# Moving dense steps between the stages of a two-layer kernel, with a new order for its mixing part

## The chip, the cores and the metric

The kernel runs on one core of a Trainium2 chip. Its time is the device time of one execution in microseconds (us), the median of the runs. The core has five engines that work beside each other, each in the order of its own instruction list: TensorE (PE) for matrix products and transposes, VectorE (DVE), ScalarE (ACT), GpSimd (POOL), and SyncE (SP), which issues most transfers. They wait for each other through semaphores.

## What is computed

Four sequences of 512 tokens with 256 features pass through two layers, all in float32. Cut to what matters:

```python
xn = layernorm(x)
# layer 0: linear attention and a gene bank, both on xn
phi = lambda a: elu(a) + 1
x = x + (phi(q) * cumsum(phi(k) * v) / 4) @ Wo.T + bo
      + tanh(ex @ Wd.T) * rms(xn) * (ex @ Wu.T) * scale   # ex: the softmax of the 32 best of 512 logits, times genes
# layer 1: a gated running mean feeding a wide dense part; and experts
xn = layernorm(x)
w = exp(rms(k)); y = sigmoid(rms(q)) * cumsum(w * v) / (cumsum(w) + 1e-6)
u, g = split(y @ w_swiglu.T)                              # 2 x 1024 wide
x = x + xn + (u * silu(g)) @ w_out.T
      + shared_expert(xn)                                 # 352 wide
      + sum of the two best of 16 experts(xn), weighted   # 176 wide each
```

## The kernel before

Tokens come in 16 tiles of 128. The program has five stages.

**Mixing**, up to the routing. Everything of layer 0, and of layer 1 the running means and the routing scores, for five units: batch 0 in two halves, and batches 1 to 3 whole. Its order on PE, DVE, ACT and POOL is fixed when the program is built. Each piece of work is a small generator (`logit_stream`, `top_stream`, `kv_stream`, `gate_stream` and others) that names the engine and an assumed duration of its next step. The class `Order` keeps a clock for each engine and lets one step go at a time: among the steps that could begin within `PULL` (line 65) of the earliest, the one with the lowest rank (`RANKS`, line 69, a number for each kind of work and unit). `LEAN` (line 106) says per unit which of two engines does a step. `begin` decides whether the normalisation of layer 1 (line 374) runs on POOL or DVE; `rise` whether ScalarE and POOL (lines 626, 629) or DVE (line 634) multiply the gene part; `value` whether ScalarE or DVE scales the values (lines 861, 867); `inverse` whether the gate's division takes two reciprocals (line 966) and one multiply into `yT` (line 990) on DVE, or one reciprocal, with POOL's product (line 962) and two further products (lines 978, 979) ahead of the multiply at line 981; `dense=27` that in the first 27 dense chunks ScalarE and POOL make `hid` (lines 1240, 1243) in place of DVE (line 1246). POOL's wide add at line 822 adds the normalised rows to `xs`. The four engines follow this order exactly; the other stages are ordered by the framework.

**Dense chunks.** The dense part and the shared expert are cut into 88 chunks: 8 halves of 256 tokens, each with `NC` = 11 chunks (3 of the shared expert, 8 of the wide part). A chunk is four products into `gu` (line 1163), a Tanh (1209; 1233 in the mixing part), two DVE operations into `hid` (1211 and 1212; 1235 and 1246 in the mixing part), and two down products into the half's accumulator `acc` (1184). The downs of a chunk stand two chunks behind its products. When a half's eleven chunks are in, DVE adds `acc` to `xs` (line 1196, `sum_up`), and the next half can have the accumulator, of which there is one. Chunks fill TensorE where other work cannot: 42 (`UPTO`) in the mixing part, the rest in the stages that follow.

**Routing** (`route`, beside 5 chunks): a product with a triangle of ones, `stri` (made at line 1038, in memory that the mixing part gives free), counts tokens per expert; DVE works out each token's row (`slot`). **Scatters** (beside 18 chunks): POOL issues 32 indirect transfers of 128 rows each (line 1138) that sort the tokens by expert in DRAM. `together` deals the two out in proportion, and `paced` ties a transfer to the last down product that was recorded before it. Three chunks follow alone.

**Experts**: 19 pairs of row groups. A step of `experts` fetches sorted rows (line 1422), turns them on TensorE (1414), copies them on ScalarE (1428), and multiplies the pair before (up 1461, Silu 1469, DVE 1470, turn, down 1483), then stores the results (1494).

**Last stage**: the remaining 20 chunks. POOL gathers the two expert rows of each token tile (32 transfers, line 1610, paced), DVE adds each to `xs` (line 1621), and SyncE stores finished tiles (1625); the last two tiles are stored after the last `sum_up` (1630). Gathers and adds are spread over the steps by the two conditions at lines 1607 and 1618.

Of the kernel before, what the change touches and what calls it, by code (L numbers as in the profile page):

```python
# [17 lines left out]
P = 128  # L18
B, L, D = 4, 512, 256
NT = L // P  # L20
# [8 lines left out]
NTT = B * NT  # L29
# [15 lines left out]
def run_all(steps):  # L45
    for _ in steps:
        pass


def together(*streams):  # L50

    live = [[iter(steps), n, 0] for steps, n in streams]
    while live:
        s = min(live, key=lambda s: s[2] / s[1])
        s[2] += 1
        if next(s[0], live) is live:
            live.remove(s)


PE, DVE, ACT, POOL = "PE", "DVE", "ACT", "POOL"  # L60
# [1 line left out]
REACH = {PE: 0.2, DVE: 0.13, ACT: 0.15, POOL: 0.1}  # L62


PULL = {PE: 0.2, DVE: 0.02, ACT: 0.05, POOL: 0.1}

RANKS = dict(
    front=(-12, 14.5, -21, -10.5, -7.5),  # L70
    turn=(-35, -36, -36, -36.5, -31.5),
    logit=(10.5, 14, 25.5, 28, 26),
    top=(-11.5, 16, 15.5, 16.5, 26),
    gene=(-46.5, -21, -41.5, -40, -30.5),
    kv=(-2, 21.5, -7.5, -8.5, 17.5),
    q=(37.5, 43, 41.5, 50, 43),
    out=(-23.5, -22.5, -5.5, -6.5, -15),
    begin=(-23.5, -26.5, -27.5, -17.5, -15.5),
    rest=(9, -28.5, -9, 4.5, -27),
    weigh=(51.5, 51, 51.5, 50.5, 52.5),  # L80
    gate=(3.5, 4, -1.5, 4.5, 9.5),
    router=(32.5, 34, 26.5, 29, 33.5),
    dense=(49, 9.5, 2),
)


# [18 lines left out]

LEAN = dict(
    taken=(1, 0, 1, 1, 1),
    rise=(0, 0, 1, 0, 0),
    norm=(0, 1, 1, 1, 1),
    value=(1, 0, 1, 1, 0),  # L110
    inverse=(1, 1, 1, 0, 0),
    begin=(0, 1, 1, 0, 1),
    dense=27,
)


class Order:
# [67 lines left out]
    def run(self):  # L185
        while self.live:
# [6 lines left out]
            if not self.live:  # L193
# [6 lines left out]
                for j, (s, t) in enumerate(zip(ready, begin))  # L200
                if s.ask[0] == engine and t <= begin[first] + PULL[engine]
            ]
# [12 lines left out]
def tile_two_layers(  # L215
# [23 lines left out]
    nc = tc.nc  # L239
# [5 lines left out]
    xs = const.tile([P, B, NT, D], F32, name="xs")  # L245
# [7 lines left out]
    def paced(inst):  # L253

        tc.add_manual_dep(
            inst,
            beat[-1],
            mybir.DependencyInfo(mybir.DependencyClass.Sync, mybir.DependencyReason.DATA),
            reason="transfers spread over the dense parts",
        )  # L260
        return inst
# [873 lines left out]
    def scatter():  # L1135
        for k in range(2):
            for i in range(NTT):
                sc = G.indirect_dma_start(  # L1138
                    out=xrows,
                    out_offset=bass.IndirectOffsetOnAxis(ap=slot[:, k, i : i + 1], axis=0),  # L1140
                    in_=xn1[:, i // NT, i % NT],
                    in_offset=None,
                ).ins
                tc.declare_no_dep(sc, group="scatter", reason="no two tokens share a row")
                tc.add_to_no_dep_group("scatter", sc)
                paced(sc)
                yield
# [9 lines left out]
    NC = len(chunks)  # L1157
    made = {}

    def up_product(gu, ins, t0, gw, g0, uw, u0, m, which, dw, dc):  # L1160
        for k, (w, at) in enumerate(((gw, g0), (uw, u0))):
            for h in range(NH):
                T.matmul(  # L1163
                    gu[0:m, k],
                    w[:, h, at : at + m],
                    ins[which][:, h, t0 : t0 + HB],
                    start=(h == 0),
                    stop=(h == NH - 1),
                )

    def source(half):

        unit = (half // 2, half % 2 * 2)
        return (unit, 0) if unit in made else ((half // 2, 0), half % 2 * HB)
# [3 lines left out]
    def down(half, n, hid):  # L1178
        nonlocal acc
        m, dw, dc = chunks[n][4], chunks[n][6], chunks[n][7]  # L1180
        if n == 0:
            acc = ps_a.tile([P, 2, D], F32, name="acc")
        for t in range(2):
            mm = T.matmul(  # L1184
                acc[:, t],
                hid[0:m, t * P : (t + 1) * P],
                dw[0:m, dc],
                start=(n == 0 and t == 0),
                stop=(n == NC - 1),
                skip_group_check=True,  # L1190
            )
        beat.append(mm.ins.name)

    def sum_up(half):
        here = xs[:, half // 2, half % 2 * 2 : half % 2 * 2 + 2]
        V.scalar_tensor_tensor(here, acc, 0.5, here, ALU.mult, ALU.add)

    def dense(first, behind):

        for c in range(first, 2 * B * NC):
            half, n = divmod(c, NC)
            unit, t0 = source(half)
            m = chunks[n][4]
            gu = ps_d.tile([P, 2, HB], F32, name="gu")
            up_product(gu, made[unit], t0, *chunks[n])
            th = wd.tile([P, HB], F32, name="th", bufs=3)
            S.activation(th[0:m], gu[0:m, 0], AF.Tanh, scale=0.5)  # L1209
            hid = wd.tile([P, HB], F32, name="hid", bufs=4)  # L1210
            V.scalar_tensor_tensor(th[0:m], th[0:m], 1.0, gu[0:m, 0], ALU.add, ALU.mult)  # L1211
            V.tensor_tensor(hid[0:m], gu[0:m, 1], th[0:m], ALU.mult)
            behind.append((half, n, hid))
            if len(behind) > 2:
                half, n, hid = behind.pop(0)
                down(half, n, hid)
                if n == NC - 1:
                    sum_up(half)
            yield
        for half, n, hid in behind:  # L1220
            down(half, n, hid)
        sum_up(half)
# [93 lines left out]
    def weight_stream():  # L1316
# [10 lines left out]
        for transfer in incoming:  # L1327
            paced(transfer)
            c += 1
            if c < UPTO:  # L1330
                yield "wait", ("down", c)

    UPTO = 42
    kinds = mybir.EngineType
    with tc.manual_schedule(engines={kinds.PE, kinds.DVE, kinds.Activation, kinds.Pool}):

# [15 lines left out]
        order.add(more_constants(), RANKS["front"][0])  # L1352
        dense_streams(order, UPTO)
        for unit, (b, i0, nt) in enumerate(((0, 0, 2), (0, 2, 2), (1, 0, NT), (2, 0, NT), (3, 0, NT))):
# [5 lines left out]
        order.run()  # L1360
    mixing.close()
    dd = dense(UPTO, [])

    def d(n):
        return islice(dd, n), n
# [1 line left out]
    routing = ctx.enter_context(ExitStack())  # L1367
    together((route(), 6), d(5))
    routing.close()
    together((scatter(), 33), d(18))  # L1370

    run_all(islice(dd, 2 * NC - 19))

    held = ctx.enter_context(ExitStack())
    wx = held.enter_context(tc.tile_pool(name="wx", bufs=2))
# [10 lines left out]
    NP2 = (NFU + NMU) // XG  # L1386
# [109 lines left out]
    def experts():  # L1496

        _, regs = nc.values_load_multi_w_load_instructions(
            offs[0:1, NTF : NTF + 2 * NMU],
            engines=[mybir.EngineType.SP],  # L1500
            min_val=0,
            max_val=(NE - 1) * EW,
            skip_runtime_bounds_check_because=clamped,
        )
        for p in range(2):
            fetch(p)
        for s in range(NP2 + 2):
            if s + 2 < NP2:
                fetch(s + 2)
            if s % every == 2 and s // every < NMU // XG:  # L1510
                bring(s // every, regs)
            if 0 <= s - 1 < NP2:
                up_tile(s - 1, 0)
            if s < NP2:
                turn_in(s)
            if 0 <= s - 1 < NP2:
                up_tile(s - 1, 1)
            if s - 2 >= 0:
                down_pair(s - 2)
            if 0 <= s - 1 < NP2:  # L1520
                turn_hidden(s - 1)
            yield
# [70 lines left out]
                    V.scalar_tensor_tensor(here, y, cpair[:, k, n : n + 1], here, ALU.mult, ALU.add)  # L1593
                nc.sync.dma_start(out[n // NT, n % NT * P : (n % NT + 1) * P], here)

    together((experts(), NP2 + 2))
    weights.close()


# [5 lines left out]
    added = 0  # L1605
    for step, _ in enumerate(dd):
        while asked < 2 * NTT and 5 * asked <= 9 * step:
            n, k = divmod(asked, 2)
            paced(
                G.indirect_dma_start(  # L1610
                    out=ys[:, asked],
                    out_offset=None,
                    in_=yrows,
                    in_offset=bass.IndirectOffsetOnAxis(ap=slot[:, k, n : n + 1], axis=0),
                ).ins
            )
            asked += 1
        while added < 2 * NTT and 15 * added <= 32 * (step - 3):
            n, k = divmod(added, 2)
            here = xs[:, n // NT, n % NT]  # L1620
            V.scalar_tensor_tensor(here, ys[:, added], cpair[:, k, n : n + 1], here, ALU.mult, ALU.add)
            added += 1
            if added % 4 == 0 and added < 2 * NTT:
                b, i = divmod(n - 1, NT)
                nc.sync.dma_start(
                    out[b, i * P : (i + 2) * P].rearrange("(t p) d -> p t d", p=P), xs[:, b, i : i + 2]
                )
    assert asked == added == 2 * NTT
    for i in (NT - 2, NT - 1):
        nc.sync.dma_start(out[B - 1, i * P : (i + 1) * P], xs[:, B - 1, i])  # L1630

# [54 lines left out]
```

## Time and profile before

| | us |
|---|---|
| median of 3 runs (526.8 to 528.15) | 526.89 |
| the profiled execution | 527.08 |
| its span, first to last instruction | 525.4 |
| TensorE busy | 506.4 |
| VectorE busy | 346.5 |
| ScalarE busy | 238.0 |
| GpSimd busy | 197.7 |
| granted TensorE clock, mean | 0.994 |

The stages stand in the span about so: mixing to 296, routing to 308, scatters and dense steps to 362.5, experts to 465, last stage to the end. In a row of the timeline the first number is the start, the second the duration, both in us; then engine, line, operation, what is written and read, and in brackets how long the engine stood idle before it and what ended that. PE is TensorE's products, PEld its weight loads. The ends of products are modelled, and consecutive ones overlap in the rows.

### The profile page before, as it was taken

The page shows a single profiled execution, that of the slowest core. Times are in us where ns is not written, and L with a number is a line of the kernel's source. Part 1 is how long each engine was busy: PE and PEld are TensorE (multiplying, and loading weights), DVE is VectorE, ACT ScalarE, POOL GpSimd, SP SyncE. Part 2 cuts the span into 40 slices and gives each one's busy share as a digit, 9 for nine tenths or more (in the row PEclk, how much of TensorE's full clock was granted, in tenths as well). Part 3 has the DMA queues.
Part 4 walks back from the last instruction along what each step waited for, and adds up shares of the span by engine and source line. Part 5 has one row for each costly group of instructions (what it writes and reads, how often), then busy time and mean ns, then how long its engine had stood idle before and what let it go on. Part 6 is the DMA issues. An engine that isn't in the chain of part 4 may idle for free.

```text
span 525.4 us, 7219 instructions
## 1 busy us (share of the span) xinstructions
PE 506.4 (96%) x2352; PEld 371.8 (71%) x2352; DVE 346.5 (66%) x938; ACT 238.0 (45%) x539; POOL 197.7 (38%) x229
## 2 busy tenths in 40 slices
PE   7899999999999999999899999999999999999895
PEld 5555575565676787678578888887776767688784
DVE  5899989999899799859559783333222222226653
ACT  2864896668757845873381111113333333311110
POOL 1713076364745566477220126660000000026562
PEclk8999999999999999999999999999999999999998
DMA  7999000000000000006516203245237345114442
GB/s 213 351 378 327 1 1 1 1 1 2 0 1 1 1 1 1 1 1 181 151 48 183 100 30 139 92 185 182 88 100 289 102 154 196 61 61 130 130 122 83
DMA packets 38920, 53.71 MB, mean 102 GB/s; under 512 B 4096, under 2 KB 33888, under 8 KB 38624
## 3 DMA queue, kind: packets, MB, share of 16 engines
q1 hardware_dynamic: 35104, 44.82, 25.2%
q0 software_dynamic: 3072, 8.39, 4.9%
q8 instruction: 20, 0.33, 0.3%
q14 instruction: 20, 0.16, 0.1%
q10 hardware_dynamic: 704, 0.01, 0.1%
HBM read 27.12 MB, written 18.61 MB: 87 GB/s over the span
## 4 chain that ended last, share of the span: by engine, by line
PE 62%; DVE 17%; POOL 8%; issue 5%; ACT 3%; DMA 2%; SPq 0%; POOLq 0%; ACTq 0%; DVEq 0%
PE gu L1163 16%; PE pu L1461 9%; PE acc L1184 8%; PE py L1483 6%; PE pm L877 6%; POOL ys L1610 5%; PE pm L413 4%; PE pt L1414 3%; PE pm L456 3%; DVE rep L560 3%; DVE top L558 2%; PE pm L380 2%; DVE sums L966 1%; PE pm L483 1%; PE pm L489 1%
## 5 line engine op out<-in xcount | busy, mean ns | idle before, releaser
L1163 PE MATMUL gu<-yT,wugt 128*128 128x256 f32 x512 | 120.4, 379 | 0.0
L1163 PEld LDWEIGHTS gu<-yT,wugt 128*128 128x128 f32 x512 | 96.3, 190 | 13.4 <-issue 0.8
L1610 POOL DMA_INDIRECT ys<-yrows,slot x32 | 30.5, 952 | 129.1 <-PE gu L1163 111.9
L1184 PE MATMUL acc<-wot,hid 128*128 128x256 f32 x256 | 66.0, 383 | 2.3 <-DVE hid L1246 1.4
L1209 ACT ACTIVATE th<-gu 128x256 f32<-128x256 f32 (+1 forms) x46 | 17.6, 383 | 103.9 <-PE gu L1163 61.6
L1184 PEld LDWEIGHTS acc<-wot,hid 128*128 128x128 f32 x256 | 47.1, 190 | 11.9 <-DVE hid L1246 2.9
L1163 PE MATMUL gu<-xn1T,sgu 128*128 128x256 f32 (+1 forms) x192 | 45.4, 380 | 0.0
L1461 PE MATMUL pu<-wex,xgT 128*128 x128 | 43.6, 463 | 1.8 <-issue 1.0
L877 PE MATMUL pm<-w,xn1T 128*128 128x512 f32 (+1 forms) x128 | 45.2, 495 | 0.0
L1211 DVE SCALAR_TENSOR_TENSOR th<-th,gu 128x256 f32<-128x256 f32 (+1 forms) x46 | 19.1, 415 | 39.1 <-ACT th L1209 27.8
L1470 DVE TENSOR_TENSOR hb<-pu,hb 128x176 f32<-128x176 f32 x38 | 13.0, 341 | 43.8 <-ACT hb L1469 43.8
L1138 POOL DMA_INDIRECT xrows<-xn,slot x32 | 31.0, 967 | 28.0 <-DVE hit L1118 11.2
L374 POOL TENSOR_SCALAR xn<-xs,mv,rs 128x256 f32<-128x256 f32 x24 | 29.3, 1233 | 27.8 <-DVE rs L754 21.1
L1163 PEld LDWEIGHTS gu<-xn1T,sgu 128*128 128x128 f32 (+1 forms) x192 | 34.5, 181 | 7.2 <-issue 1.0
L413 PE MATMUL pm<-xnT,wqkv 128*128 128x512 f32 x72 | 33.9, 598 | 0.0
L877 PEld LDWEIGHTS pm<-w,xn1T 128*128 128x128 f32 x128 | 23.5, 190 | 14.4 <-issue 10.7
L558 DVE MAX8 top<-rep 128x8 f32<-128x512 f32 x48 | 32.8, 683 | 0.3
L560 DVE MATCH_REPLACE8 rep<-top,rep 128x512 f32<-128x512 f32 x48 | 32.4, 675 | 0.0
L456 PE MATMUL pm<-wct,xnT 128*128 128x512 f32 x64 | 31.8, 620 | 0.3 <-ACT lg L517 0.2
L1474 DVE COPY hgT<-pt 128x512 f32<-128x512 f32 x19 | 13.1, 692 | 28.6 <-PE pt L1414 28.6
L1483 PE MATMUL py<-wex,hgT 128*128 x128 | 30.6, 382 | 0.0
L1233 ACT ACTIVATE th<-gu 128x256 f32<-128x256 f32 (+1 forms) x42 | 16.0, 383 | 31.9 <-PE gu L1163 30.8
(205 smaller groups left out, 946.6 us busy)
## 6 DMA issues: line engine op xcount, KB each, us to landing
xrows<-zero SPq DMA_DIRECT2D x1, 6016.0 KB
wex<-in_w_gate_up_dram SPq DMA_DIRECT2D x8, 704.0 KB, 5.0
xn<-wex SPq DMA_DIRECT2D x9, 608.0 KB, 4.3
xg<-xrows SPq DMA_DIRECT2D x19, 256.0 KB, 2.8
yrows<-yg SPq DMA_DIRECT2D x19, 256.0 KB, 2.1
wugt<-in_wug_dram SPq DMA_DIRECT2D x1, 2048.0 KB
wex<-in_w_down_dram SPq DMA_DIRECT2D x4, 512.0 KB
w<-wex SPq DMA_DIRECT2D x3, 608.0 KB
```

The costliest lines, as they stand in the source:

```text
L374: engine.tensor_scalar(to, xs[:, b, i], mv[:, 0:1], rs[:, 0:1], ALU.subtract, ALU.mult)
L413: T.matmul(pm, wqkv[:, h, c * P : (c + 1) * P], k.xnT[:, h, tok], start=(h == 0), stop=(h == NH - 1),)
L456: T.matmul(pl, k.xnT[:, h, i * P : (i + 1) * P], wct[:, h], start=(h == 0), stop=(h == NH - 1))
L558: V.max(tp[:, 8 * r : 8 * r + 8], src)
L560: V.match_replace(rep, tp[:, 8 * r : 8 * r + 8], src, TAKEN)
L877: T.matmul(po[:, 0:n], g.xnT[:, h, i * P : (i + 1) * P], w1[:, h, 0:n] if o == "q" else w1[:, h, 2 * D : 2 * D + n], start=(h == 0), stop= ...
L1138: sc = G.indirect_dma_start(out=xrows, out_offset=bass.IndirectOffsetOnAxis(ap=slot[:, k, i : i + 1], axis=0), in_=xn1[:, i // NT, i % NT] ...
L1163: T.matmul(gu[0:m, k], w[:, h, at : at + m], ins[which][:, h, t0 : t0 + HB], start=(h == 0), stop=(h == NH - 1),)
L1184: mm = T.matmul(acc[:, t], hid[0:m, t * P : (t + 1) * P], dw[0:m, dc], start=(n == 0 and t == 0), stop=(n == NC - 1), skip_group_check=True,)
L1461: T.matmul(pg[rows, 0 : 2 * NI], pairs[p]["xT"][:, i, h, rows], w[:, bass.ds(at + h * 2 * NI, 2 * NI)], start=(h == 0), stop=(h == NH - 1),)
L1483: mm = T.matmul(py[rows, i * D : (i + 1) * D], hT[:, i, h, rows], w[:, bass.ds(at + EW - (2 - h) * D, D)], start=(h == 0), stop=(h == 1),)
L1610: G.indirect_dma_start(out=ys[:, asked], out_offset=None, in_=yrows, in_offset=bass.IndirectOffsetOnAxis(ap=slot[:, k, n : n + 1], axis=0) ...
```

## The change

- The tables: `PULL` of POOL from 0.1 to 0.2; nearly all `RANKS` by small amounts; in `LEAN` `rise` for the last unit, `value` and `begin` and `inverse` for some units, `dense` from 27 to 18.
- `UPTO` from 42 to 40: two chunks fewer in the mixing part.
- 17 chunks beside the scatters instead of 18 (still 3 alone after them).
- One chunk is put behind the first step of `experts`, which turns the first rows.
- The last stage so has 22 chunks. Its adds go by another rule, and at the very last chunk the waiting down products are left to the end of the loop.
- The last of the two final stores is issued by ScalarE.

```diff
-PULL = {PE: 0.2, DVE: 0.02, ACT: 0.05, POOL: 0.1}
+PULL = {PE: 0.2, DVE: 0.02, ACT: 0.05, POOL: 0.2}
...
-    begin=(-23.5, -26.5, -27.5, -17.5, -15.5),
-    rest=(9, -28.5, -9, 4.5, -27),
+    begin=(-15, -27, -16.5, -14, -11),
+    rest=(8.5, -23, -10.5, 5.5, -28),
...
-    dense=(49, 9.5, 2),
+    dense=(49, 9, 2.5),
...
-    rise=(0, 0, 1, 0, 0),
+    rise=(0, 0, 1, 0, 1),
     norm=(0, 1, 1, 1, 1),
-    value=(1, 0, 1, 1, 0),
-    inverse=(1, 1, 1, 0, 0),
-    begin=(0, 1, 1, 0, 1),
-    dense=27,
+    value=(1, 1, 1, 0, 0),
+    inverse=(0, 1, 1, 1, 1),
+    begin=(0, 1, 1, 0, 0),
+    dense=18,
...
-            if len(behind) > 2:
+            if len(behind) > 2 and c < 2 * B * NC - 1:
...
-    UPTO = 42
+    UPTO = 40
...
-    together((scatter(), 33), d(18))
-
-    run_all(islice(dd, 2 * NC - 19))
+    together((scatter(), 33), d(17))
+
+    run_all(islice(dd, 3))
...
-    together((experts(), NP2 + 2))
+    pairwise = experts()
+    next(pairwise)
+    next(dd)
+    run_all(pairwise)
...
-        while added < 2 * NTT and 15 * added <= 32 * (step - 3):
+        while added < 2 * NTT and added < 2 * (step - 5):
...
-    for i in (NT - 2, NT - 1):
-        nc.sync.dma_start(out[B - 1, i * P : (i + 1) * P], xs[:, B - 1, i])
+    for i, queue in ((NT - 2, nc.sync), (NT - 1, nc.scalar)):
+        queue.dma_start(out[B - 1, i * P : (i + 1) * P], xs[:, B - 1, i])
```

## What the change was predicted to do

> **What bounds the kernel now.** I read the page's engine rows first, then the slices, then the timeline around each place where TensorE stands still.
>
> ```profile
> span 525.4 us, 7219 instructions
> ...
> PE 506.4 (96%) x2352; PEld 371.8 (71%) x2352; DVE 346.5 (66%) x938; ACT 238.0 (45%) x539; POOL 197.7 (38%) x229
> ...
> PE   7899999999999999999899999999999999999895
> ```
>
> TensorE (PE) is busy in 96% of the span, and no slice between the first and the last falls below 8 tenths. The change keeps every product, so time can only come out of TensorE's standstills, or go into new ones. I count a standstill from start to start: in a running dense step products of 256 columns start every 0.216 us per record (eight records in 1.73 us, a whole step of 12 records in 2.59 us), while one record is shown as 0.38 us. So the idle time that a row shows is about 0.17 us short of what was lost.
>
> The timeline has five standstills that the change can touch. First, where the experts begin:
>
> ```profile
> 362.55 0.60 PE L1414 MATMUL pt<-ident,xg 128*128 128x128 f32 x4
> ...
> 363.26 0.58 ACT L1428 COPY xgT<-pt 128x512 f32<-128x512 f32 x1 [0.99 <-PE pt L1414]
> 363.87 1.28 ACT L1469 ACT_TABLE_LOAD   x1
> ...
> 363.90 1.45 PE L1461 MATMUL pu<-wex,xgT 128*128 x4 [0.75 <-ACT xgT L1428]
> ```
>
> The first expert product waits for ScalarE's copy of the turned rows: 0.75 shown, 0.92 us lost. Next, in the last stage:
>
> ```profile
> 493.79 0.48 DVE L1621 SCALAR_TENSOR_TENSOR xs<-ys,cpair,xs 128x256 f32<-128x256 f32 x1 [1.26 <-DMA ys<-yrows,slot]
> 494.20 0.41 DVE L1212 TENSOR_TENSOR hid<-gu,th 128x256 f32<-128x256 f32 x1
> ...
> 494.53 0.68 DVE L1196 SCALAR_TENSOR_TENSOR xs<-acc,xs 128x512 f32<-128x512 f32 x1
> ...
> 495.27 0.92 PE L1184 MATMUL acc<-sdn,hid 128*128 128x256 f32 x3 [1.54 <-DVE xs L1196]
> ```
>
> VectorE (DVE) works in order. An add at L1621 waits 1.26 us for its gathered rows; the dense `hid` and the sum L1196 queue behind it, and the next half's first down product cannot have the accumulator: 1.71 us lost. The same thing closes the kernel, costing 0.75 us (0.58 shown):
>
> ```profile
> 517.70 0.48 DVE L1621 SCALAR_TENSOR_TENSOR xs<-ys,cpair,xs 128x256 f32<-128x256 f32 x1 [0.51 <-DMA ys<-yrows,slot]
> 518.10 0.42 DVE L1212 TENSOR_TENSOR hid<-gu,th 128x256 f32<-128x256 f32 x1
> ...
> 518.57 1.13 PE L1184 MATMUL acc<-wot,hid 128*128 128x256 f32 x4 [0.58 <-DVE hid L1212]
> 519.74 0.69 DVE L1196 SCALAR_TENSOR_TENSOR xs<-acc,xs 128x512 f32<-128x512 f32 x1 [1.22 <-PE acc L1184]
> 520.46 1.07 SPq L1630 DMA_DIRECT2D out_dram<-xs  x2
> ```
>
> The other two lie in the mixing part that the rank tables order:
>
> ```profile
> 250.05 2.36 POOL L822 TENSOR_TENSOR xs<-xs,xn 128x1024 f32<-128x1024 f32 x1
> 250.16 2.79 DVE L990 TENSOR_TENSOR yT<-sums 128x512 f32<-128x512 f32 x1
> ...
> 253.34 0.92 PE L1184 MATMUL acc<-wot,hid 128*128 128x256 f32 x3 [1.36 <-DVE hid L1246]
> ```
>
> ```profile
> 295.41 0.20 POOL L1038 MEMSET stri<- 128x128 f32 x1 [21.82 <-DVE yT L990]
> ...
> 296.06 0.70 PE L1053 MATMUL pr<-chosen,stri 128*128 128x256 f32 x2 [0.62 <-POOL stri L1039]
> ```
>
> A 2.79 us multiply, 0.69 us long when alone (289.93), costs TensorE 1.53 us. And the routing's first product waits for `stri`, whose memory is free only after the last unit's last `yT`: 0.79 us.
>
> **Part by part: the last stage.** 22 steps stand here in place of 20, which moves two chunks and adds nothing. The gathers keep their rate of 1.8 a step (POOL 1.27 us each, 2.3 of 2.59 us), so the last is still asked for at step 18. The adds change from 2.13 a step from step 3 to two a step from step 6. Before, add 31 was queued at step 18, beside its own gather; now at step 21. A gather takes 2.8 us from issue to landing and the lag is some three steps, 7.8 us, so no add should find its rows missing. What VectorE then has per step is 0.41 + 0.42 + 2 x 0.48 = 1.8 us, with the sum 2.5 us, within 2.59. So I give back 1.71 + 0.75 = 2.46 us. Each output store (2.9 us to landing) goes some steps later; the seventh is asked for at step 19, over 5 us before the end. The condition on the last step leaves TensorE's order as it is in the built program (last up product, then three pairs of downs): 0.
>
> **The last store.** Its two halves go to SP's and ScalarE's queues. SP's issues take 0.35 and 0.66 us, the second starting 0.40 us after the first; the teardown waits for both. ScalarE has nothing else left. Bounds: 0.4 us gained, or 0 and slightly below if the first store's landing is what counts; I take 0.2.
>
> **The dense step behind the first turned rows.** TensorE gets 8 + 4 records (2.59 us) between the transposes at 362.55 and the first expert product. They hide the copy (0.58 us plus its hops): 0.92 us back. ScalarE gets a Tanh (0.38) between copy and first Silu, VectorE its pair (0.83); both end before the first expert product does. SP's order does not change. A rule speaks against this edit: by "ScalarE: Activation LUTs", section "What ACT_TABLE_LOAD costs", every switch of table set costs some 2.66 us with its drain, so a Tanh placed among Silus could pay two switches, 5.3 us. The trace says otherwise: one load of 1.28 us stands before the first Silu, and the Tanh at 465.26, the first after the Silus, follows without one; in the built program the Tanh goes ahead of that one load. By the rule taken blindly the edit would lose 4.4 us, by the row it gains 0.92; I take the row.
>
> **17 steps beside the scatters.** In the built program 137 products of 0.432 us stand between the routing's product pair and the turned rows, where 151 stood: 60 us with that pair, where the trace has 66.5. The rows are needed 6.5 us sooner. The slots are known some 10.5 us after the routing's product; 32 scatters at 1.27 us (2.4 us of each 2.59 us step) reach the last, which is paced by a down product 7.8 us before the turns. From it 2.45 us pass to the fetch (355.20 to 357.65 before) and 2.8 us to landing: 2 us to spare, as before. Cost 0; without that cover it would be a microsecond or so.
>
> **Forty chunks and new ranks.** From this trace's rows the edited tables change VectorE's mixing work by -3.8 us (four reciprocals fewer, -7.0; seven more `hid` multiplies, +2.8; the rest small), ScalarE's by -3.5 and POOL's by 0. TensorE's order differs only from about 110 us on. Though two chunks move out, the same 424 up products stand before the routing's product, and only two pairs of downs fewer (1.7 us).
>
> The tail can be worked out. From the last unit's first projection (255.61 before) to the routing's product TensorE now has 10.5 us of projections, 37 up products (16.0), 7 pairs of downs (6.05) and 24 transposes (2.6): 35.2 us, where the trace has 39.7. The chain beside it: turns of the weights at +19.2, first scan at +19.8; then on VectorE four scans (4.84), two combinations (1.34), two reciprocals (3.48), two multiplies (1.36) and nine dense pieces (3.5), 14.5 us; twice a multiply waits for POOL's two (0.77 + 0.72), of which dense pieces cover 0.8 and 0.4: 1.8 us. That is +36.1, and 0.8 us to `stri` as before: +36.9. TensorE waits 1.7 us where it waited 0.79: +0.9 us.
>
> The body, 110 us to the tail, has 2.9 us of standstills now. The 1.53 goes if POOL's wide add no longer meets a multiply; but other pairs are newly side by side. "SBUF — State Buffer", section "SBUF: two separate sides", says that a VectorE operation with two SBUF inputs and a POOL one take turns, each waiting for the other's whole instruction. The row at 250.16 agrees; the multiplies moved to POOL at two more units (six passes of about 0.74 us each, 4.5 us a unit) are what the rule turns against. By the rule's worst reading each unit loses 4.5 us; but `yT` waits for its own passes anyway, and scans and dense pieces take an input from PSUM. The multiplies at 199.6 and 204.5, the nearest rows, took 0.68 and 1.20 us. Bounds: -2.9 and +4.5; I take 0.
>
> **Sum** against the profiled execution, 527.08 us (span 525.4 and 1.7 around it): -2.46 - 0.2 - 0.92 + 0.9 + 0 = -2.7, so 524.4. The median shown is 0.2 below that execution: 524.2.
>
> **The rivals.** *The mixing gains too*: its order was the cause of 2.9 us; if half goes and the tail chain is no longer than TensorE's work, 522.2. For it: VectorE has 3.8 us less to do. Against: the tail's arithmetic. *The mixing takes the gain back*: one hold like the one at 250 us at each of the two changed units, some 2.2 us, gives 526.4, or the adds merely move the wait to another row. *Slower*: in the last two units' gates, POOL's passes and VectorE's take turns. The last unit's 4.5 us fall wholly on the chain to `stri`, half of the other's, 2.2, on TensorE: 524.4 + 6.7, about 531. It decides once TensorE loses over 4.3 us more than I assume between 110 us and the routing's product. Against it: between 187 and 205 us, where one unit works this way already, TensorE lost 0.44 us.
>
> **How the numbers follow.** A measurement of this kernel tells about 0.3% from no change: 1.6 us, so 525.3 to 528.5. Forecast 524.2 (522.8 to 525.3): 0.50. Mixing gains, 522.2: 0.17. Gain taken back, 526.4: 0.20. Slower, 531: 0.13. Faster 0.67, the same 0.20, slower 0.13. The range 521.8 to 527.2 leaves out the slower case and the far end of the gain.
>
> **What would show it.** In the profile after: no idle time worth the name before the first expert product; no add waiting for a gather and no idle at the accumulator's change in the last stage; the last down product directly behind its neighbours; the routing's product waiting 1 to 2 us for `stri`. I am wrong if TensorE stands still for over 4 us between 110 us and the routing, if the turned rows wait for the scatters, or if a second table load appears beside the moved step.

## The result and the profile after

On record the changed kernel takes 531.38 us (median of 6 runs, 529.9 to 533.48), the kernel before beside it 527.69 (6 runs, 526.8 to 528.63): a ratio of 1.0078, 95% interval 1.005 to 1.0105. It is slower by 3.7 us where a gain of 2.7 was predicted. The profiled execution took 533.48 us, the longest of the six and 2.1 us over the median, so the losses read from it are on the high side. Its page, in the lines that answer to those of before, and one group of it:

```profile
span 531.8 us, 7220 instructions
...
PE 509.1 (96%) x2352; PEld 373.9 (70%) x2352; DVE 343.0 (65%) x945; ACT 237.3 (45%) x532; POOL 198.1 (37%) x232
...
PE   6899999999999999999999999699999999999895
...
PEclk8999999999999999999999999799999999999999
...
L1184 PE MATMUL acc<-sdn,hid 128*128 128x256 f32 (+1 forms) x96 | 26.1, 399 | 6.4 <-DVE xs L1196 4.9
```

The share of TensorE is 96% as before, and does not show the loss. The slices say where to look: one digit inside the kernel has fallen to 6 (about 332 to 346 us), and the clock granted to TensorE falls to 7 tenths just there. The group names the wait: first down products of a half, waiting for the sum of the half before.

The timeline of that stretch, among the scatters (in brackets: how long the engine was idle, and what ended it):

```profile
332.69 1.24 PE L1163 MATMUL gu<-xn1T,sgu 128*128 128x256 f32 x5
...
334.63 1.89 PE L1163 MATMUL gu<-xn1T,sgu 128*96 128x256 f32 x8
...
339.22 0.65 ACT L1209 ACTIVATE th<-gu 128x256 f32<-128x256 f32 x2 [6.76 <-remote]
339.52 0.96 POOL L1138 DMA_INDIRECT xrows<-xn,slot  x1 [2.34 <-remote]
...
340.43 0.68 DVE L1196 SCALAR_TENSOR_TENSOR xs<-acc,xs 128x512 f32<-128x512 f32 x1
...
341.17 2.07 PE L1184 MATMUL acc<-sdn,hid 128*128 128x256 f32 x4 [4.65 <-DVE xs L1196]
...
343.03 3.62 PE L1163 MATMUL gu<-yT,wugt 128*128 128x256 f32 x8
```

Read it from the bottom. TensorE idles 4.65 us before the first down product of half 5 (4.81 lost, start to start), since it waits for `sum_up` (L1196). (A half is 11 chunks; half 5 begins with chunk 55, whose downs stand behind the products of chunk 57.) The sum was late because VectorE works in order and the `hid` of chunk 56 stands ahead of it. That `hid` waited for ScalarE's Tanh, and the Tanh is the odd row: the products of chunk 56 are shown to end at 332.69 + 1.24 = 333.93 (the row has the last five of its eight records), and nothing else held ScalarE, yet the Tanh starts at 339.22, **5.29 us late**. Chunk 57's products end at 336.52, its Tanh starts 2.98 us late, in the same row. GpSimd, whose next scatter is paced by a down product of 334.8, gets on 0.3 us later, at 339.52. Three events of TensorE thus became visible to two engines within 0.3 us, several us after the products. The trace's records of TensorE's semaphore say the same: none between 332.78 and 339.20 us, then three within 0.15 us. So it is the signal that was late, and not its readers that were slow. I call this a late signal: the difference between the shown end of a chunk's up products and the start of its Tanh, where ScalarE was free. Normally it is 0.04 us.

Behind the idle the clock is low: eight records take 3.62 us where they took 1.89. A row of the table of stretches shows it too (columns: stretch, its length, busy time and count of PE, PEld, DVE, ACT, POOL, then granted clock, DMA share, GB/s):

```profile
341.00:350.00 9.00, 8.83 (x28) 7.37 (x29) 1.92 (x6) 0.77 (x2) 4.48 (x5) 0.68 0.32 127
```

From 341.2 to 346.5 a record of 256 columns takes 0.43 us in place of 0.216; 13 of them cost 2.8 us. The Trainium skill, "TensorE: Matmul & The Clock Gate", section "What's actually happening", says that TensorE falls to half its clock after an idle window of about 3.4 us and needs as long a busy one to come back. This case agrees in kind: 4.65 us idle, half clock for 5.3 us. The bill of this place is 4.8 + 2.8 = 7.6 us, more than the whole loss of 6.4 us of span between the two profiles.

Was it there before? The same chunks in the kernel before, ScalarE alone:

```profile
333.73 0.38 ACT L1209 ACTIVATE th<-gu 128x256 f32<-128x256 f32 x1 [2.88 <-PE gu L1163]
338.04 0.38 ACT L1209 ACTIVATE th<-gu 96x256 f32<-96x256 f32 x1 [3.93 <-PE acc L1184]
```

Yes. Among its scatters five Tanhs were late, 6.8 us in sum, at most 2.43 (the second row here: chunk 57, products ended at 335.61). TensorE lost 0.23 us by it. In the changed kernel the sum is 14.9 us and the longest 5.29.

The rest of the change, in the rows that answer to the prediction's. Where the experts begin:

```profile
362.98 0.60 PE L1415 MATMUL pt<-ident,xg 128*128 128x128 f32 x4
...
363.70 0.59 ACT L1429 COPY xgT<-pt 128x512 f32<-128x512 f32 x1 [0.99 <-PE pt L1415]
...
365.35 0.39 ACT L1209 ACTIVATE th<-gu 128x256 f32<-128x256 f32 x1 [1.07 <-PE gu L1163]
365.75 1.28 ACT L1470 ACT_TABLE_LOAD   x1
...
366.01 1.35 PE L1462 MATMUL pu<-wex,xgT 128*128 x4
```

No idle is left before the expert product, and one table load stands behind the Tanh. The last stage at the accumulator's change, and its end:

```profile
500.25 0.48 DVE L1625 SCALAR_TENSOR_TENSOR xs<-ys,cpair,xs 128x256 f32<-128x256 f32 x1 [0.53 <-DMA ys<-yrows,slot]
...
502.05 0.68 DVE L1196 SCALAR_TENSOR_TENSOR xs<-acc,xs 128x512 f32<-128x512 f32 x1
...
502.78 1.13 PE L1184 MATMUL acc<-sdn,hid 128*128 128x256 f32 x4 [1.56 <-DVE hid L1212]
```

```profile
526.40 0.69 DVE L1196 SCALAR_TENSOR_TENSOR xs<-acc,xs 128x512 f32<-128x512 f32 x1 [1.29 <-PE acc L1184]
527.12 0.35 SPq L1634 DMA_DIRECT2D out_dram<-xs  x1
527.12 0.37 ACTq L1634 DMA_DIRECT2D out_dram<-xs  x1
```

Adds still wait for gathers, and the accumulator's change still costs 1.72 us. At the end the twelve down records of the last three chunks run without a gap (523.61 to 526.36), and both stores go out at once: from the end of the sum to the end of the span 4.71 us (527.09 to 531.8), where it was 4.97. The end of the mixing part:

```profile
293.76 0.29 POOL L1039 TENSOR_SCALAR_AFFINE_SELECT stri<-stri 128x128 f32<-128x128 f32 x1
...
294.11 0.70 PE L1053 MATMUL pr<-chosen,stri 128*128 128x256 f32 x2 [1.31 <-POOL stri L1039]
```

The product waits 1.31 us for `stri` (1.47 lost). Counted from start to start, TensorE loses 5.85 us between 110 us and here, where it lost 6.96.

### The profile page after: what moved, and what is told of

Same layout as the page of the kernel before. It is cut to its first block, busy times and chain, and to the rows that moved or that the text cites. A ratio compares the mean times of both kernels' runs of the same rounds, so it can differ in the third digit from the quotient of the medians.

```text
span 531.8 us, 7220 instructions
## 1 busy us (share of the span) xinstructions
PE 509.1 (96%) x2352; PEld 373.9 (70%) x2352; DVE 343.0 (65%) x945; ACT 237.3 (45%) x532; POOL 198.1 (37%) x232
## 4 chain that ended last, share of the span: by engine, by line
PE 65%; DVE 20%; POOL 6%; issue 4%; DMA 2%; another core or an unknown queue 1%; ACT 1%; SPq 0%; POOLq 0%; DVEq 0%; ACTq 0%
PE gu L1163 20%; PE acc L1184 11%; PE pu L1462 9%; PE py L1484 6%; PE pm L877 6%; PE pt L1415 3%; DVE rep L560 3%; POOL ys L1614 3%; DVE top L558 3%; PE pm L380 2%; PE pm L456 2%; DVE phi L430 2%; DVE cum L442 1%; PE pm L413 1%
## 5 line engine op out<-in xcount | busy, mean ns | idle before, releaser
L1163 PE MATMUL gu<-yT,wugt 128*128 128x256 f32 x512 | 122.8, 383 | 0.0
L1163 PEld LDWEIGHTS gu<-yT,wugt 128*128 128x128 f32 x512 | 97.4, 192 | 14.5 <-issue 1.4
L1209 ACT ACTIVATE th<-gu 128x256 f32<-128x256 f32 (+1 forms) x48 | 18.2, 384 | 115.9 <-PE gu L1163 59.3
L374 POOL TENSOR_SCALAR xn<-xs,mv,rs 128x256 f32<-128x256 f32 x20 | 24.5, 1239 | 27.1 <-DVE rs L754 17.6
L1184 PE MATMUL acc<-sdn,hid 128*128 128x256 f32 (+1 forms) x96 | 26.1, 399 | 6.4 <-DVE xs L1196 4.9
L541 POOL TENSOR_TENSOR e<-e,rep 128x512 f32<-128x512 f32 x14 | 18.0, 1289 | 36.9 <-ACT rep L538 36.9
```

Of the source, the lines that this page charges most:

```text
L374: engine.tensor_scalar(to, xs[:, b, i], mv[:, 0:1], rs[:, 0:1], ALU.subtract, ALU.mult)
L1163: T.matmul(gu[0:m, k], w[:, h, at : at + m], ins[which][:, h, t0 : t0 + HB], start=(h == 0), stop=(h == NH - 1),)
L1184: mm = T.matmul(acc[:, t], hid[0:m, t * P : (t + 1) * P], dw[0:m, dc], start=(n == 0 and t == 0), stop=(n == NC - 1), skip_group_check=True,)
```

## The experiments

Seventeen runs in five groups. The kernels of a group ran on the same chip, with the kernel before among them; all ratios are to that. By the record's numbers the chips were 5, 11, 12, 11 and 3, so the second and the fourth group name the same one. "Beside" counts the dense steps dealt out with the scatters.

### First group: is it the 17 steps, and is it GpSimd? (before: 527.85 us)

**e1**, the changed kernel with 18 steps beside and two after:

```diff
-    together((scatter(), 33), d(17))
-    run_all(islice(dd, 3))
+    together((scatter(), 33), d(18))
+    run_all(islice(dd, 2))
```

> The changed kernel with 18 dense steps beside the scatters again and two alone after them; all else as changed. Theory 'bursts': while GpSimd issues one indirect transfer directly behind another (10 in a row in the changed kernel, at most 8 before), TensorE's signals reach the other engines late; with 17 steps GpSimd needs 2.4 of every 2.59 us and never falls idle, so the late signals last 5.3 us and stop TensorE for 4.8 us at the accumulator's change, and the clock falls to half for 5 us more (2.9 us). With 18 steps the late signals stay near the 2.4 us of the kernel before: about 525 us (523.5 to 526.5), no idle over 1 us between 309 and 362 us. Rival 'boundary': the accumulator's change now falls on the tenth step beside the scatters instead of the eighth, and any late signal there stops TensorE; 18 steps leave it at the tenth, so the stall stays: 530 to 533 us. Rival 'tables': the new order of the mixing part is the cause of the loss: about 531 us too, but without the idle at the change of the accumulator.

531.65 us, ratio 1.007 (1.005 to 1.009). The stall stays (3.35 us, with half clock behind it; late signals up to 4.20). My first theory, that 17 steps do it by packing GpSimd too full, falls; "boundary" has it right.

**e2**, the kernel before with 17 steps beside and four after:

> The kernel before with 17 dense steps beside the scatters and four after them, nothing else changed. Theory 'bursts': late signals of 4 us and more, and a stall of TensorE among the scatters: 529 to 534 us, against 527.7 for the kernel before. Rival 'boundary': the accumulator's change stays at the eighth step, so the time stays: 527 to 528.5 us. By the prediction's own step (17 steps cost nothing, 2 us to spare): 527 to 528.5 us.

528.6 us, ratio 1.0018 (1.0006 to 1.003). Late signals up to 4.49 us, but the stalls are small (0.44 at the accumulator's change, 0.82 later). So 17 steps cost 0.75 us here (by the interval 0.3 to 1.6), which the prediction had put at nothing; that longer late signals are the reason rests on one profile of each.

**e3**, the changed kernel with the line `paced(sc)` taken out:

> The changed kernel with the scatters not tied to the down products, so GpSimd issues them one directly behind another, 32 x 1.27 = 41 us in a row. Theory 'bursts': TensorE's signals are late through most of these 41 us; stalls of several us each, 540 us or more. Rival 'starved': the late signals are an effect of GpSimd waiting for TensorE, not of the issuing: without the tie there are none, the scatters end some 5 us sooner, and the time is 523 to 526 us.

551.9 us, ratio 1.0463 (1.0439 to 1.0487). GpSimd issues all 32 scatters from 304.0 to 344.6 us in one row. ScalarE in that stretch (lines one lower, as one was taken out):

```profile
315.76 0.38 ACT L1208 ACTIVATE th<-gu 128x256 f32<-128x256 f32 x1 [3.75 <-remote]
325.63 0.38 ACT L1208 ACTIVATE th<-gu 128x256 f32<-128x256 f32 x1 [9.49 <-remote]
349.56 0.94 ACT L1208 ACTIVATE th<-gu 128x256 f32<-128x256 f32 x3 [23.55 <-remote]
355.68 0.38 ACT L1208 ACTIVATE th<-gu 128x256 f32<-128x256 f32 x1 [5.18 <-PE gu L1162]
```

Three Tanhs start together 5 us after the last scatter; the oldest of their products had been ready for 30.2 us, and TensorE stood still for 18 us. In this group GpSimd's row of transfers and the late signals belong together; the waiting of GpSimd is not their cause, "starved" is out.

**e4**, the changed kernel with one expert's 16 scatters, one a step; the other 16 are left out, so the second expert's rows stay zero:

> The changed kernel with only the first expert's 16 scatters (the second expert's 16 are left out, so their rows stay zero), one beside each of the 17 dense steps; TensorE's work is the same. Theory 'bursts': GpSimd is idle for half of every step, no signal is late, no idle over 0.5 us between 309 and 362 us: 523 to 525.5 us. If the late signals come from elsewhere (TensorE's own code loading, weights loaded at the same time): the stall of 4.8 us stays, 530 to 533 us.

523.95 us, ratio 0.9932 (0.9913 to 0.995). No late signal among the scatters, no stall. On the same chip, with the signals in time, the change gains 3.6 us (2.6 to 4.6) where 2.7 was predicted, though this kernel also has 16 issues less.

### Second group: which part brings the stall? (before: 527.81 us)

**e5**, the kernel before with the changed tables (`PULL`, `RANKS`, `LEAN`) and `UPTO = 40`, nothing else:

> The kernel before with the changed tables and 40 dense chunks up to the routing, nothing else changed (18 and 3 steps, 22 in the last stage, old rule for the adds, both last stores on SyncE). Theory 'a pair ahead': the change of the accumulator at chunk 44 now falls on the first scatters; the downs of chunks 44 and 45 come close together (0.9 us), so GpSimd trails the downs that pace it by one step, always holds the permission for two more transfers, issues 10 in a row, and the late signals last 4 us and more where the next change of the accumulator stands: a stall of 3 to 5 us and slow clock behind it: 530 to 532.5 us, late signals of 4 us or more in the profile. Rival 'the rest of the change': the tables only make the mixing part 1 to 2 us shorter, the stall comes from the other edits: 526 to 527 us.

531.49 us, ratio 1.0061 (1.0044 to 1.0078). Tables and chunk count alone bring a loss as large, within the intervals: 3.37 us of stall, then slow clock.

```profile
339.54 1.20 PE L1184 MATMUL acc<-sdn,hid 128*128 128x256 f32 x4 [3.21 <-DVE xs L1196]
340.53 3.55 PE L1163 MATMUL gu<-yT,wugt 128*128 128x256 f32 x8
```

**e6**, the changed kernel with the old tables and 42 chunks (adds from step 3, as 20 steps are left):

> The changed kernel with the old tables and 42 chunks (17 steps beside the scatters, three after, one behind the first turned rows, 20 in the last stage with the adds from step 3 at two a step, the last store on ScalarE). Theory 'a pair ahead': late signals as in the kernel before with 17 steps (528.6 us in its run), no long stall; less 0.9 us where the experts begin and 0.1 to 0.2 at the end: 527 to 528 us. Rival 'the rest of the change': 530 us or more.

528.51 us, ratio 1.0012 (1.0002 to 1.0021). A little over what was expected: 1.23 us at the accumulator's change, 0.54 before the turned rows, which wait for the scatters here, and the idle at the end (0.70) is back, with 20 steps in the last stage. The other edits are not what stops TensorE for over 3 us.

**e7**, the changed kernel with one of the three later steps put ahead of the scatters:

> The changed kernel with one of the three steps behind the scatters put ahead of them, so that each scatter is tied to a down product one step later; the work is the same. Theory 'a pair ahead': GpSimd waits for its down products again and stands still as soon as a signal is late; late signals under 2.5 us, no stall over 1 us at the change of the accumulator: 524.5 to 527 us, perhaps 0.5 us at the turned rows. Rival 'boundary': any late signal at the change of the accumulator stops TensorE for 3 to 5 us: 530 to 532 us.

530.62 us, ratio 1.0046 (1.0031 to 1.0061). The late signal on chunk 56 (3.74 us) and the stall (3.26) stay, and 2.18 us are added where the turned rows now wait for the scatters. "A pair ahead" falls too.

**e8**, the changed kernel with VectorE's order in the last stage taken from the source:

```diff
-    for step, _ in enumerate(dd):
-        ...
+    with tc.manual_schedule(engines={kinds.DVE}):
+        for step, _ in enumerate(dd):
+            ...
```

> The changed kernel with VectorE's order in the last stage fixed to the order of the source (two adds behind each step's hid from step 6 on). In the changed kernel's profile every add follows its own gather by 1.8 to 3.2 us whatever the rule says, since the framework puts it there. Theory 'order': with the source's order no add waits, and the 1.7 us at the accumulator's change in the last stage go: 1.7 us under the changed kernel's 531.4, about 529.7 us (528.5 to 531), and no idle over 0.3 us there. Rival: the sum waits for something else (late signals among the gathers): 531 us, the idle stays.

529.89 us, ratio 1.0034 (1.0016 to 1.0051): 1.5 us under the changed kernel on record, with a stall of 4.29 us among the scatters. The last stage at its accumulator's change:

```profile
498.35 0.68 DVE L1196 SCALAR_TENSOR_TENSOR xs<-acc,xs 128x512 f32<-128x512 f32 x1
...
499.08 1.13 PE L1184 MATMUL acc<-sdn,hid 128*128 128x256 f32 x4
```

The down product follows the sum at once and no idle is left, though signals were late in this stage too (2.29 us at most). "Order" holds: the new rule for the adds took nothing off this wait because the framework, not the source, orders VectorE there. In the changed kernel's trace each add starts 1.8 to 3.2 us after the issue of its own gather has ended, in that of before 1.8 to 2.7 us.

### Third group (e9 to e12) and fourth (e13 to e15): the place of the late signal (before: 526.24 and 525.94 us)

A sharper form of "boundary" was left. A late signal stops TensorE at once only on the second chunk of a half (chunk 56): its `hid` stands ahead of the sum, and the next down product needs the sum. On any other chunk TensorE has two steps in hand (in the changed kernel 4.21 us on chunk 51 cost 0.54). With 40 chunks ahead, chunk 56 is the twelfth step beside the scatters and is hit; with 42 it is the tenth, and chunk 57 was hit. (The expectation of e1 counts chunk 54, the last of half 4: the tenth and the eighth.) The profiles on record and those of the first two groups bear it out. Where the scatters begin at chunk 45 or 46, chunk 56 is 3.7 to 5.3 us late (the changed kernel, e1, e5, e7, e8), and where they begin at 47, about 0.7 us (the kernel before, e2, e6); e3 and e4 issue otherwise and stand outside this.

**e9**, e5 with two steps more ahead of the scatters, so that they begin at chunk 47 as before:

```diff
+    run_all(islice(dd, 2))
     together((scatter(), 33), d(18))
```

> The kernel before with the changed tables and 40 chunks, and two more dense steps between the routing and the first scatter, so that the scatters begin at chunk 47 as before (20 steps in the last stage, as before). Theory 'place of the late signal': the long late signal comes on the tenth to twelfth step beside the scatters in every kernel; it stops TensorE only where it falls on the second chunk of a half (chunk 56), whose hid stands ahead of the sum on VectorE, and the next down product waits for that sum. With 40 chunks ahead chunk 56 is the twelfth step, with 42 the tenth. Two steps ahead bring it back to the tenth: the late signal falls on the next chunk, the idle is 0.2 to 1 us, and the shorter mixing is left: 526 to 527.5 us. Rival 'tables': if the new order itself causes the late signals, 530 to 532 us as with the tables alone (531.5).

**e10** and **e11**, the changed kernel and the kernel before with a second accumulator for halves 4 and 7:

```diff
-            acc = ps_a.tile([P, 2, D], F32, name="acc")
+            acc = extra[half]() if half in extra else ps_a.tile([P, 2, D], F32, name="acc")
...
+    ps_b = second.enter_context(tc.tile_pool(name="ps_b", bufs=1, space=bass.MemoryType.PSUM))
+    extra[4] = lambda: ps_b.tile([P, 2, D], F32, name="acc")
...
+    extra[7] = lambda: ps_x.tile([P, L], F32, name="py").rearrange("p (t d) -> p t d", t=2)
```

> The changed kernel with a second accumulator in PSUM for half 4 and for half 7, so that the first down product of half 5 and of half 7 needs no sum of the half before; all else is as changed. Theory 'place of the late signal': the signals are late as before (4 to 5 us), but TensorE runs on: the 4.8 us, the 2.9 us of slow clock behind it and the 1.7 us in the last stage go: 531.4 - 9.4 = 522.0; about 1 us may stand where a late signal outlasts the two steps that TensorE has in hand: 521 to 524 us. Rival: if TensorE itself stands still in the stretch where its signals are late, the time stays at 530 us or more.

> The kernel before with the same second accumulators. Theory: 0.2 us among the scatters and 1.7 us in the last stage go: 527.8 - 1.9 = 525.9 us (525 to 526.8). Then the rest of the change would be worth 525.9 - 522 = 3 to 4 us, once its stall is out. If the waits at the changes of accumulator merely move to the next product: 527 to 528 us.

**e12**, e10 with 20 steps beside the scatters and two after, 20 in the last stage:

> The changed kernel with second accumulators, 20 steps beside the scatters and two behind them (20 left in the last stage). Theory: GpSimd needs 2.0 of 2.59 us, the late signals are shorter (under 3 us) and what is left of their cost goes: 0.3 to 1 us under the kernel with second accumulators alone, 521 to 523 us. Rival: the scatters end three steps later and the turned rows wait for them: 1 to 3 us over it.

e9: 525.31 us, ratio 0.9979 (0.9966 to 0.9993). e10: 522.38, 0.9924 (0.9907 to 0.9941). e11: 525.16, 0.9972 (0.9956 to 0.9987). e12: 523.55, 0.9943 (0.9926 to 0.9961); its turned rows wait for nothing, but with 20 steps in the last stage 0.75 us of idle at the end is back. The times look like a proof, and are none: **not one signal was late in any of these four profiles**, although e10 issued all 32 scatters in one row. e10 met its forecast without the late signals that the forecast assumed, which is luck. So the kernel's pattern alone does not make them late. The changed kernel was run again, with the most telling one beside it.

> The changed kernel itself, once more. In the third group of runs no kernel shows a single late signal, even with 32 scatters in a row, and the kernel before ran 1.6 us faster beside it than beside the first two groups. Theory 'occasion': late signals come with the chip or the occasion, not with the kernel's issue pattern alone. If this group has none, the changed kernel takes 3 to 4 us less than on record, about 523.5 us where the kernel before takes 526.2, a ratio of 0.994 to 0.996, with no idle over 0.5 us among the scatters and 1.0 to 1.7 us left in the last stage. If this group has them, 531 us against 527.8 with the stall as before. Theory 'pattern': the third group's kernels lacked them by their own issue pattern: 531 us against 526 to 528 here in any case.

> The changed kernel without the tie between scatters and down products, once more (551.9 us the first time, with signals up to 30 us late). Theory 'occasion': where the group has no late signals, the 32 scatters in a row cost nothing and it takes what the changed kernel takes, 523 to 524 us; where it has them, about 552 us. Theory 'pattern': about 552 us in any case.

> The changed kernel with second accumulators, once more. If this group has no late signals: 1.0 to 1.7 us under the changed kernel in the same group. If it has them: the stall at the accumulator's change goes though the signals are late, 522 to 525 us, 6 to 9 us under the changed kernel; if TensorE itself stands still while its signals are late, no gain over 2 us.

e13, the changed kernel itself: **523.28 us, ratio 0.9954 (0.9941 to 0.9967)**. e14, not paced: 522.94, 0.9952 (0.9937 to 0.9966), where it had been 551.9. e15, second accumulators: 521.95, 0.9927 (0.9914 to 0.994). e14's ScalarE in the stretch shown for e3:

```profile
341.97 0.38 ACT L1208 ACTIVATE th<-gu 128x256 f32<-128x256 f32 x1 [2.21 <-PE gu L1162]
344.56 0.38 ACT L1208 ACTIVATE th<-gu 128x256 f32<-128x256 f32 x1 [2.21 <-PE gu L1162]
```

A Tanh every 2.59 us, like a clock, beside 32 scatters in one row. "Occasion" holds: the same program has late signals in one group and none in another, and the second group had them on a chip of the same number.

### Fifth group: the cure where it matters (before: 527.83 us)

e10 and e9 once more, in a group that did have late signals:

> The changed kernel with second accumulators, a third time, in the hope of a group with late signals; its profile shows whether there are any. If there are (ScalarE's Tanh over 2 us behind its products): the stall at the accumulator's change is gone and it takes 522 to 525 us where the changed kernel took 531.4 and the kernel before 527.8, a ratio of 0.99 to 0.995; if TensorE itself stands still while its signals are late, 529 us or more, a ratio over 1. If there are none: 522 us and 0.993, as in the two groups without.

> The kernel before with the changed tables and two dense steps ahead of the scatters, again. If there are late signals: the long one falls on chunk 57 instead of 56 and the stall is 0.2 to 1 us, a ratio to the kernel before of 0.996 to 1.0, where the tables alone had 1.006. If the tables call the late signals up wherever they fall: 1.004 to 1.008. If there are none: 0.998, as before.

e16: 525.63 us, ratio 0.996 (0.9945 to 0.9974), a little over the 522 to 525 that were expected. Signals are later here than in the changed kernel on record (up to 6.41 us, 20.3 in sum), and at the accumulator's change (334.29) TensorE runs on; it stops where one signal outlasts its two steps:

```profile
334.29 1.03 PE L1185 MATMUL acc<-sdn,hid 128*128 128x256 f32 x4
...
345.74 1.67 PE L1163 MATMUL gu<-yT,wugt 128*128 128x256 f32 x7
349.99 1.13 PE L1185 MATMUL acc<-wot,hid 128*128 128x256 f32 x4 [2.58 <-DVE hid L1213]
```

e17: 526.88 us, ratio 0.998 (0.9969 to 0.9991). Chunk 56 was late by 0.75 us, and TensorE lost 0.52 us there:

```profile
334.99 1.13 PE L1184 MATMUL acc<-sdn,hid 128*128 128x256 f32 x4 [0.35 <-DVE xs L1196]
```

The same tables with the scatters two chunks earlier (e5) took 1.0061. So both cures hold where signals are late: take the sum out of the way, or move the place.

| kernel | late among the scatters: sum, longest | lost at the change of accumulator | ratio to before |
|---|---|---|---|
| before | 6.8, 2.43 | 0.23 | 1 |
| changed, on record | 14.9, 5.29 | 4.81 | 1.0078 |
| e5, tables, scatters from chunk 45 | 10.3, 3.85 | 3.37 | 1.0061 |
| e17, tables, scatters from chunk 47 | 5.7, 2.33 | 0.52 | 0.998 |
| e16, changed, second accumulator | 20.3, 6.41 | 0 (2.75 elsewhere) | 0.996 |
| e13, changed, no late signals | 0, 0.04 | 0 | 0.9954 |

### What else differs between the groups

In the seven profiles of the third and fourth group each scatter leaves 16 records of its semaphore in the trace, 512 in all. The eleven others with 32 scatters hold 84 to 215, and the two with the latest signals, e3 and e16, hold the fewest (84 and 122). e4, in time among its 16 scatters, holds 232 of 256. So where TensorE's signals come late, most of these records of the profiler are missing too. Every time on record comes from an execution with a profiled span; there is none without the profiler. So a rival stands untested: that on some occasions the recording itself holds the signals back, so that the loss, or part of it, would go where nothing is recorded. A third thing could also be behind both.

## Why the prediction was wrong

**The term that was missing.** Signals of TensorE arrive late among the scatters, and how much that costs depends on which chunk they hit. The prediction has no term for it. Its sentence on forty chunks, that two chunks move out and "only two pairs of downs fewer" stand before the routing's product, counted the work and not the place: chunk 56 went from the tenth to the twelfth step beside the scatters. In the groups with late signals this turned -2.7 us into +3.7 (e5 has it alone, e17 takes it back). The trace of before showed the lateness (338.04), but as TensorE lost only 0.23 us by it there, it was passed over.

**The sum of the rest was right, not each term, and so in part by luck.** In the group without late signals the change takes the time from 525.94 to 523.28 us, -2.66 (by the interval -1.7 to -3.1); the sum on record was -2.7. The kernel before was not profiled in such a group, so the terms below mix profiles with and without late signals:
- *Expert start, -0.92*: right; the idle is gone, one table load, as the row and not the rule had it.
- *Last stage, -1.71*: the step failed. It took the source's rule for VectorE's order. The framework places each add by its own reckoning, and the rule moved nothing (1.72 us still lost); with the order taken from the source (e8) the idle goes. Without late signals 0.40 us is lost there (e13), with the old rule and 20 steps 0.94 (e9): 0.5 less, with a cause that was not looked into.
- *The end, -0.75*: the gain came, by another cause. The old rule gives it as well with 22 steps (e5), and 20 steps bring it back (e6, e12). It is the length of the stage behind the last gather.
- *Last store, -0.2*: 0.26 in this profile; but e6 and e12, which store on two queues after 20 steps, end as late after the sum as the kernel before, so that the second queue alone brings it is not shown.
- *17 steps, 0*: the rows did not wait (362.98), yet e2 loses 0.75 us, and in e6 they do wait, 0.54 us. The size is near the "microsecond or so" without cover; late signals are the likely cause, and not the one given.
- *Mixing, +0.9*: the tail's wait of 1.7 us came out at 1.47, so +0.7 of it. The body was put at 0 and gave 1.8 us: the 1.53 at 251.7 us is gone. Other pairs did meet (VectorE's L450 took 1.63 us at 110.03 in place of 0.68, beside POOL's L541; `yT` 1.11 us at 152.1 in place of 0.40), and the one TensorE stop seen behind them is 0.44 us, at 113.03. In all TensorE loses 1.1 us less where 0.9 more was forecast: the rival "the mixing gains too", in direction and size. All 15 profiles with the new tables repeat it: from the last record that both orders share, at 111 us, to the routing's product they take 182.1 to 182.2 us where the old tables take 185.0, and 1.73 of that are the two pairs of downs moved out. (Of the "424 up products" ahead of that product the trace shows 338 records, the same in both kernels.)
- *Left out*: with 40 chunks an accumulator's change falls into the routing, where VectorE is busy, and TensorE loses 0.39 us (308.84). All eleven profiles with 40 chunks and one accumulator show it, and none with 42.

The terms as measured, -0.92 - 0.5 - 0.75 - 0.26 - 1.1 + 0.39, make -3.1, at the edge of the interval: a last stage that gained less than forecast was made up by a mixing part that gained where a loss was forecast.

**The rival "slower"** had the right time, 531, and the wrong place. GpSimd's passes did not meet VectorE's in the last gates (`yT` took 0.69 us at 288.97 and 292.62). None of the three signs named for being wrong appeared either.

What stays open: why signals are late in some groups and not in others, whether the recording has a part in it, and by which path GpSimd's transfers and TensorE's late signals are tied. The runs show that both belong together where signals are late (e3, e4) and that the program alone does not decide it (e13 to e15).

## What to carry to other kernels

Compare, beside indirect transfers from GpSimd, the shown end of a product with the start of its first reader; lateness that costs nothing today is a debt that falls due when another edit moves a hand-over with no slack, such as the change of a single accumulator, onto it. Give that hand-over slack (a second buffer) before tuning the rest. Run the same kernel on several occasions before one result is believed. And take an engine's order from the built program where a framework orders it: a rule in the source may move nothing.

## What was not expected of the hardware

- While GpSimd issues indirect transfers in a row, TensorE's completions can reach other engines up to 6 us late, 30 us in the extreme (e3), and then several at once; in other groups of the same programs 0.04 us is the most. The Trainium skill, "Perfetto Trace Analysis", section "Tensor Engine Instruction (MATMUL, LD_WEIGHTS)", says that TensorE's end is estimated and that its signal comes after PSUM's acknowledgement; with signals in time a reader starts 0.04 us after the shown end here, so the estimate does not make the lateness. That TensorE itself had gone on is shown by e16, where it lost nothing at the accumulator's change.
- Half clock after a stop of TensorE: after 4.81 us lost at once, and after 3.35 us in e1 at once too; after 3.37 and 3.26 us in e5 and e7 about a us later and for some 3 us; after 2.75 us not (e16).
